# Context products of layer 2 in one unit of sixteen per half, nine probability buffers, and a new set of places

## The chip, the cores and the metric

The kernel runs on one core of one Trainium2 chip. The metric is the device time of one execution in microseconds (us); the number of a kernel is the median of its runs. The kernel before takes 3557.0 us (three runs, 3556.24 to 3559.87).

## The reference

There are 32 graphs of 512 nodes with 256 features in fp32, each with a symmetric adjacency matrix. Four graph layers follow one another, and each is wrapped as `x = layernorm(x + layer(x, adj))`. Layers 0, 1 and 3 are graph attention layers with additive logits. Layer 2 is a transformer block with masked attention over eight heads of 32, and it is the one that is changed:

```python
scores = einsum('bhqd,bhkd->bhqk', q * scale, k)
scores = where(allowed[:, None], scores, -inf)
attn = softmax(scores, axis=-1)
ctx = einsum('bhqk,bhkd->bhqd', attn, v)
x = layernorm(x + ctx @ Wo.T + bo)
x = layernorm(x + relu(x @ W1.T) @ W2.T)
```

## The kernel before

**Tiling.** A batch is one graph. Its 512 nodes are four row tiles of 128 (R = 4, index `j` or `r`), its 256 features two halves of 128 (K = 2, index `c`). Each half of layer 2 holds four heads. TensorE does the products and transposes, ScalarE (ACT) the exponentials and the copies out of PSUM, VectorE (DVE) masks, sums and statistics. Everything on the way from one layer to the next stays in SBUF, except the q and k of layer 2, which go over a DMA.

**Order.** A batch is a Python generator (`graph`), which yields a number, its place, before each unit of TensorE work. The place is `PERIOD * b + PLACES[stage][i]`, with the table in lines 28 to 48, and a merge by these numbers (`heapq.merge`) puts the units of several batches in one order. For TensorE this order is kept as it is (`manual_schedule`). The orders of ScalarE, VectorE and the DMA queue are set by the tile framework's scheduler. In the steady part, one period of 106.5 us holds the work of one batch, but of stages from different batches: layers 0 and 1 of a later batch run between the attention, feed forward and layer 3 of earlier ones.

**Names in the trace.** All products go through one helper, so they all carry line L104 and are told apart by their PSUM tiles: `h0p`, `h1p`, `h3p` are the features times weights of layers 0, 1, 3; `gp` spreads logits by transposes; `o` and `den` are the attention sums (`o<-pt,hv` and `den<-pt,hv` of layer 0 are column-tiled, 32 columns wide, four heads abreast; `o<-h,pt` are layers 1 and 3); `backp`, `xt1p`, `xt2p`, `xt3p`, `ytp` are transposes; `qkp` and `vp` make q, k and v; `s` are scores; `cp` are context products; `den<-pr,ones` are the sums of probabilities; `wop` is the projection; `f1p` and `f2p` are the feed forward.

**Attention of layer 2** (function `attention`). For each half `c`, and each row tile `j` and pair of heads `hp` in it, two products make scores `s` of 128x512; at `j = 3` a bf16 product adds the mask `shut` to them. ScalarE takes the exponential of each into a tile `pr` of 128x2x512 (L622). For `j < 3` VectorE multiplies that tile with the mask (L625). The context products read `pr` and `v` and accumulate in one PSUM bank `cp` per half, in four column tiles of 32, one per head. Before the change they are two units of eight per half, one after `j = 1` and one after `j = 3`, and the bank is taken at the half's start. After each unit VectorE adds the `pr` tiles of the two row tiles pairwise (`add_to`, L652). The halves of these sums are added later (`add_halves`), then `divide` multiplies with ones (`den`), takes the logarithm and exponential on ScalarE (L594 to L596), and scales the context `ct` on VectorE (L599). ScalarE's copy of `cp` to `ct` is L644.

**Buffers.** PSUM has one tag of eight banks (`bank`), which all products share in turn. `pr` has seven buffers. The `part` tag (128x512 scratch) has nine buffers in the first stage of a batch and six in the third.

**Other lines that the steps touch.** L280 normalises `y` on ScalarE with `rs` from L265, L266 (ScalarE) and L276 (VectorE), after the statistics `bn` (L273, L274). L421 is the exponential behind `h0p` that `gp` needs. L349 copies `gp` to `gb`, and L407 makes the layers' attention tiles `pt` from `gb` on VectorE. L695 is the activation `ft` between `f1p` and `f2p`. L709 to L711 add `f2p` to the second layernorm's `y`.

Of the kernel before, what the change touches and what calls it, by code (L numbers as in the profile page):

```python
# [9 lines left out]
F32 = mybir.dt.float32  # L10
# [15 lines left out]

PERIOD = 12054
PLACES = {
    "edges": [-3978, -1691, -957, 174],
    "x": [5375],  # L30
    "mask": [15529, 15550, 17375, 20858],
    "layer 0": [
        -32810, -32810, -32810, -32129, 5406, 5406, 5406, 5452, 8379, 10181, 10354, 11030,
        12979, 12979, 12979,
    ],
    "layer 1": [15397, 15397, 15551, 15551, 15637, 16368, 16395, 17082, 17350, 17359, 17359, 17361],
    "qkv": [17440, 17444, 22256, 22270, 23119, 23902, 25371, 25371, 25371, 25371, 25371],
    "attention": [
        -2905, -2905, -2905, -1865, 26410, 26425, 26425, 26425, 26478, 26596, 27423, 27447,
        27455, 27460, 28382, 28382, 28780, 28780, 29468, 30180, 32292, 32292, 33750, 33750,  # L40
    ],
    "projection": [34383, 34383, 34383, 34383, 35158],
    "feed forward": [
        35968, 36004, 36525, 37429, 38387, 38478, 38499, 38551, 38551, 38733, 38733, 39509,
        39509, 39647, 39706, 40498, 41141, 41450, 41519,
    ],
    "layer 3": [44306, 44306, 45121, 45121, 46359, 46359, 46477, 48020, 48020, 48023, 48398, 48528],
}
STAGES = {"edges": "a", "x": "a", "layer 0": "a", "layer 1": "a", "feed forward": "c", "layer 3": "c"}
ALL = mybir.DependencyInfo(mybir.DependencyClass.Sync, mybir.DependencyReason.DATA)  # L50
# [22 lines left out]
def fast_path(ctx: ExitStack, tc: tile.TileContext, a: dict, out: bass.AP, bad: bass.AP):  # L73
# [8 lines left out]
    nc = tc.nc  # L82
    B, N, D = a["x"].shape
    P = 128
    R = N // P
# [4 lines left out]
    DH = D // H2  # L90
# [12 lines left out]
    def product(what, *args, **kwargs):  # L103
        latest[0] = what(*args, **kwargs).ins.name  # L104
# [35 lines left out]
    v = const.tile([P, R, D], F32, name="v")  # L140
# [30 lines left out]
    def weights0():  # L171
        load_w(w0, "w0t")
        ab = part("a0")
        bcast(ab, "a0")
        bcast(bias0, "bias0")

        for s in range(2):
            prod = part("prod").rearrange("p (k d) -> p k d", k=K)
            nc.vector.tensor_mul(
                prod, w0[:, :, :D], ab[:, s * D : (s + 1) * D].unsqueeze(1).to_broadcast([P, K, D])  # L180
            )
            for k in range(K):
                nc.vector.tensor_reduce(
                    w0[:, k, D + s * H : D + (s + 1) * H],
                    prod[:, k, :].rearrange("p (h e) -> p h e", h=H),
                    axis=X,
                    op=ALU.add,
                )

    def weights13(w, name, vectors):  # L190
        load_w(w, name)
        ab = part(vectors)
        bcast(ab, vectors)
        for s in range(2):
            prod = part("prod").rearrange("p (k d) -> p k d", k=K)
            nc.vector.tensor_mul(
                prod, w[:, :, :D], ab[:, s * D : (s + 1) * D].unsqueeze(1).to_broadcast([P, K, D])
            )
            nc.vector.tensor_reduce(w[:, :, D + s], prod, axis=X, op=ALU.add)
# [45 lines left out]
    sb = ctx.enter_context(tc.tile_pool(name="sb", bufs=1))  # L245
    ps = ctx.enter_context(tc.tile_pool(name="ps", bufs=2, space=bass.MemoryType.PSUM))
    stage = ["a"]

    def buf(shape, tag, name, bufs, dtype=F32):

        return sb.tile(shape, dtype, tag=tag + stage[0], name=name, bufs=bufs)

    def bank(name, dtype=F32):
        shape = [P, 2048 // (2 if dtype == BF16 else 4)]
        return ps.tile(shape, dtype, tag="mm", name=name, bufs=8)

    def part(name):

        return buf([P, N], "part", name, {"a": 9, "c": 6}[stage[0]])

    def all_rows(v):
        return v.unsqueeze(1).to_broadcast([P, R, D])
# [312 lines left out]
    def attention(qk, a2, shut, spread):  # L575
        ct = buf([P, K, N], "ct", "ct", 1)
        pr = []

        def add_halves(pr):
            for hp in range(2):  # L580
                add_to(pr[0][hp], pr[2][hp])

        def divide(c, sums):
            den = bank("den")
            for hh in range(4):
                product(nc.tensor.matmul,
                    den[hh * DH : (hh + 1) * DH, :],
                    ones,
                    sums[hh // 2][:, hh % 2, :],
                    start=True,  # L590
                    stop=True,
                )
            t = buf([P, N], "dens", "dens", 2)
            nc.scalar.activation(t, den, AF.Copy, accum_out=spread[:, 2 * c : 2 * c + 1])  # L594
            nc.scalar.activation(t, t, AF.Ln)
            nc.scalar.activation(  # L596
                t, t, AF.Exp, scale=-1.0, accum_out=spread[:, 2 * c + 1 : 2 * c + 2]
            )
            nc.vector.tensor_mul(ct[:, c, :], ct[:, c, :], t)  # L599

        for c in range(K):
            cp = bank("cp")
            last, pr = pr, []
            for j in range(R):
                pr.append([])
                for hp in range(2):
                    yield
                    if last and (j, hp) == (1, 0):
                        add_halves(last)
                    t = sb.tile([P, 2, N], F32, tag="pr", name="pr", bufs=7)  # L610
                    for i in range(2):
                        s = bank("s")
                        product(nc.tensor.matmul,
                        s,
                            qk[2 * c + hp][:, 1, i, j * P : (j + 1) * P],
                            qk[2 * c + hp][:, 0, i, :],
                            start=True,
                            stop=j < R - 1,
                        )
                        if j == R - 1:  # L620
                            product(nc.tensor.matmul, s, identb, shut, start=False, stop=True)
                        nc.scalar.activation(t[:, i, :], s, AF.Exp, scale=QSCALE)  # L622
                    if j < R - 1:
                        edges = a2[:, j, :].unsqueeze(1).to_broadcast([P, 2, N])
                        nc.vector.tensor_mul(t, t, edges)  # L625
                    pr[j].append(t)
                if j % 2 == 0:
                    continue
                yield
                for jj in (j - 1, j):  # L630
                    for hh in range(4):
                        product(nc.tensor.matmul,
                        cp[hh * DH : (hh + 1) * DH, :],
                            v[:, jj, (4 * c + hh) * DH : (4 * c + hh + 1) * DH],
                            pr[jj][hh // 2][:, hh % 2, :],
                            start=jj == 0,
                            stop=jj == R - 1,
                        )
                for hp in range(2):
                    add_to(pr[j - 1][hp], pr[j][hp])  # L640
                if last and j == 1:
                    yield
                    divide(0, last[0])
            nc.scalar.copy(ct[:, c, :], cp)  # L644
        yield
        add_halves(pr)
        yield
        divide(1, pr[0])
        return ct

    def add_to(t, u):
        nc.vector.tensor_add(t, t, u)  # L652
# [830 lines left out]
```

## Time and profile before

| Quantity | Value |
|---|---|
| median of 3 runs | 3557.0 us (3556.24 to 3559.87) |
| profiled execution, its own time | 3556.76 us |
| its span | 3555.0 us |
| TensorE, products busy | 3422.4 us (96%) |
| TensorE, weight loads busy | 2385.6 us (67%) |
| VectorE busy | 2909.0 us (82%) |
| ScalarE busy | 2227.6 us (63%) |
| DMA queue q1, share of 16 engines | 33.6% |
| one period, from a context unit to the same one of the next batch (1498.79 to 1605.33 us) | 106.54 us |

The profile is of one execution. Busy times are sums over an engine's instructions. Products on TensorE overlap one another and their ends are modelled, so short pauses between them don't all show as idle time; they show in the starts. A line of the timeline is a run of equal instructions: its start, its length from the first start to the last end, engine, line, operation, output and inputs, shape, number, and in brackets an idle time ahead of it with what ended it. Each fp32 product shows as two records, a transpose as one.

### The profile page before, as it was taken

What the parts mean: (1) busy time and instruction counts of PE and PEld (TensorE: products, weight loads), DVE (VectorE), ACT (ScalarE), POOL (GpSimd) and SP (SyncE); (2) the same over time, 40 slices, a digit from 0 to 9 for tenths busy, and PEclk for the clock granted to TensorE, in tenths of its full rate; (3) what the DMA queues carried; (4) which work ended last, traced back from release to release, by engine and by line L of the source; (5) the groups of instructions that cost most, each with busy time, mean ns of one, the idle gap of its engine ahead of it and who ended that gap; (6) DMA issues with size and microseconds to landing.
All of it is one profiled execution on the core that took longest, in us unless ns stands there. A gap on an engine that the chain in (4) does not pass through costs nothing.

```text
span 3555.0 us, 51660 instructions
## 1 busy us (share of the span) xinstructions
PE 3422.4 (96%) x18278; PEld 2385.6 (67%) x18342; DVE 2909.0 (82%) x5178; ACT 2227.6 (63%) x5441; POOL 83.3 (2%) x171
## 2 busy tenths in 40 slices
PE   5899999999999999999999999999999999999986
PEld 3466666776666776666776666776666776676655
DVE  5788888888888888888888888888888888888763
ACT  3556666666666666666666666666666666666653
POOL 0000000000000000000000000000000000000000
PEclk8999999999999999999999999999999999999999
DMA  4334232334332234332334332334333234332120
GB/s 129 83 75 89 68 78 66 70 77 90 69 78 67 68 77 90 70 76 68 67 77 90 71 76 68 67 78 90 71 75 69 66 78 89 72 75 64 41 54 13
DMA packets 164040, 261.03 MB, mean 73 GB/s; under 512 B 20416, under 2 KB 56384, under 8 KB 163776
## 3 DMA queue, kind: packets, MB, share of 16 engines
q1 hardware_dynamic: 163776, 257.65, 33.6%
q8 instruction: 149, 2.44, 0.3%
q14 instruction: 115, 0.94, 0.1%
HBM read 106.57 MB, written 16.78 MB: 35 GB/s over the span
## 4 chain that ended last, share of the span: by engine, by line
PE 83%; DVE 10%; ACT 6%; DMA 1%; issue 1%; SPq 0%; ACTq 0%; DVEq 0%
PE o L104 14%; PE f2p L104 13%; PE f1p L104 12%; PE cp L104 7%; PE qkp L104 6%; PE s L104 6%; PE den L104 5%; PE h1p L104 3%; PE h3p L104 3%; PE wop L104 3%; PE vp L104 3%; DVE bn L273 3%; ACT y L280 2%; PE backp L104 1%; DVE relu L521 1%; DVE y L711 1%
## 5 line engine op out<-in xcount | busy, mean ns | idle before, releaser
L407 DVE SCALAR_TENSOR_TENSOR pt<-gb,ex,at 128x512 f32<-128x512 f32 x768 | 534.9, 740 | 51.3 <-ACT gb L349 48.8
L622 ACT ACTIVATE pr<-s 128x512 f32<-128x512 f32 x1024 | 537.4, 614 | 35.3 <-PE s L104 29.6
L652 DVE TENSOR_TENSOR pr<-pr 128x1024 f32<-128x1024 f32 x384 | 451.6, 1216 | 113.5 <-PE cp L104 113.1
L104 PE MATMUL f2p<-wf,ft 128*128 128x256 f32 x2048 | 491.3, 383 | 5.1 <-ACT ft L695 5.1
L625 DVE TENSOR_TENSOR pr<-pr,a 128x1024 f32<-128x1024 f32 x384 | 452.5, 1219 | 45.9 <-ACT pr L622 42.8
L104 PE MATMUL f1p<-yt,wf 128*128 128x256 f32 x2048 | 484.0, 379 | 2.4 <-ACT yt L320 0.2
L104 PE MATMUL o<-h,pt 128*128 128x257 f32 x2048 | 474.6, 381 | 5.4 <-DVE pt L407 3.8
L104 PEld LDWEIGHTS f2p<-wf,ft 128*128 128x128 f32 x2048 | 380.0, 189 | 110.8 <-issue 27.7
L104 PEld LDWEIGHTS o<-h,pt 128*128 128x128 f32 x2048 | 383.3, 190 | 75.8 <-issue 21.1
L695 ACT ACTIVATE ft<-f1p,cols 128x256 f32<-128x256 f32 x512 | 217.9, 471 | 342.6 <-PE f1p L104 339.0
L104 PEld LDWEIGHTS f1p<-yt,wf 128*128 128x128 f32 x2048 | 388.9, 190 | 54.5 <-ACT yt L320 0.7
L280 ACT ACTIVATE y<-y,rs 128x256 f32<-128x256 f32 x768 | 398.6, 593 | 11.2 <-DVE rs L276 11.1
L104 PE MATMUL s<-qk 128*128 128x512 f32 x1024 | 350.6, 458 | 4.4 <-DMA qk<-lo 2.1
L273 DVE BATCH_NORM_STATS2 bn<-y 128x6 f32<-128x256 f32 x768 | 298.3, 412 | 5.6
L104 PE MATMUL cp<-pr,v 128*32 128x512 f32 x2048 | 290.4, 609 | 2.6 <-ACT pr L622 1.1
L104 PE MATMUL o<-pt,hv 128*32 128x512 f32 x2048 | 279.9, 595 | 6.9 <-DVE pt L407 6.9
L104 PE MATMUL qkp<-xt,wqkv 128*128 128x512 f32 x512 | 233.6, 599 | 0.0
L104 PEld LDWEIGHTS s<-qk 128*128 128x128 f32 x1024 | 192.7, 191 | 36.5 <-issue 5.6
L548 DVE SCALAR_TENSOR_TENSOR lo<-qkp,cols,hi 128x512 fp32r<-128x512 f32 x128 | 95.6, 747 | 127.9 <-ACT hi L547 119.9
L349 ACT COPY gb<-gp 128x512 f32<-128x512 f32 x192 | 105.9, 586 | 125.5 <-PE gp L104 125.0
L104 PEld LDWEIGHTS qkp<-xt,wqkv 128*128 128x128 f32 x512 | 94.3, 189 | 121.3 <-issue 118.6
L104 PEld LDWEIGHTS o<-pt,hv 128*32 128x32 f32 x2048 | 87.1, 109 | 131.5 <-issue 77.4
(139 smaller groups left out, 4699.2 us busy)
## 6 DMA issues: line engine op xcount, KB each, us to landing
qk<-hi SPq DMA_DIRECT2D x512, 128.0 KB, 3.9
qk<-lo SPq DMA_DIRECT2D x512, 128.0 KB, 4.2
adjt<-in_adjt SPq DMA_DIRECT2D x64, 512.0 KB, 4.1
adj<-in_adj SPq DMA_DIRECT2D x64, 512.0 KB, 4.9
xt<-in_xt SPq DMA_DIRECT2D x32, 512.0 KB, 3.8
x<-in_x SPq DMA_DIRECT2D x32, 512.0 KB, 6.3
out<-y SPq DMA_DIRECT2D x32, 512.0 KB, 4.7
wf<-in_w1t SPq DMA_DIRECT2D x1, 1024.0 KB, 8.6
```

Of the source, the lines that this page charges most:

```text
L104: latest[0] = what(*args, **kwargs).ins.name
L273: nc.vector.bn_stats(st[:, r, :], y[:, r, :])
L280: nc.scalar.activation(y[:, r, :], y[:, r, :], AF.Identity, bias=rs[:, 1, r : r + 1], scale=rs[:, 0, r : r + 1],)
L349: nc.scalar.copy(g, p)
L407: nc.vector.scalar_tensor_tensor(t, g, f, edges, op0=ALU.max, op1=ALU.mult)
L521: nc.vector.scalar_tensor_tensor(y, m, 1.0, y, op0=ALU.min, op1=ALU.add)
L548: nc.vector.scalar_tensor_tensor(lo, p, bias, hi.bitcast(F32), op0=ALU.add, op1=ALU.subtract)
L622: nc.scalar.activation(t[:, i, :], s, AF.Exp, scale=QSCALE)
L625: nc.vector.tensor_mul(t, t, edges)
L652: nc.vector.tensor_add(t, t, u)
L695: nc.scalar.activation(ft[:, f, :], p[:, f, :], AF.Relu, bias=bf1[:, ff + f : ff + f + 1])
L711: nc.vector.tensor_mul(y, y, all_rows(ln2g))
```

## The change

- Per half, the context products become one unit of sixteen, after all four row tiles, and `cp` takes its bank only there. The four pairwise additions follow that unit. The place between `j = 1` and the division of the first half's context stays.
- `pr` gets nine buffers instead of seven.
- The third stage's `part` tag gets five buffers instead of six.
- `dynamic_dma_scratch_size` goes from 8192 to 512.
- `PLACES` has new numbers in all stages; `attention` has 22 instead of 24, one for each unit.
- From the attention function on, line numbers are smaller by one: L622, L625, L644, L652, L695 before are L621, L624, L643, L651, L694 after.

What this makes of TensorE's order in a steady period, from the order in which the changed program's instructions stand: the first half's sixteen come after its last scores and between feed-forward units, as the second of its two units did. The second half's sixteen come directly behind its last scores and ahead of `xt3p`; before, eight stood with `den<-pr,ones` in the stretch of the first half's division, and eight behind `xt3p` and ahead of layer 0's first `o`. Layer 0's `o` and `den` for `j = 1` come behind `den<-pr,ones`, and for `j = 0` behind `xt3p`, with six of the eight `h3p` and `xt2p` between.

```diff
 PLACES = {
-    "edges": [-3978, -1691, -957, 174],
+    "edges": [-6012, -1639, -513, 645],
...
     "attention": [
-        -2905, -2905, -2905, -1865, 26410, 26425, 26425, 26425, 26478, 26596, 27423, 27447,
-        27455, 27460, 28382, 28382, 28780, 28780, 29468, 30180, 32292, 32292, 33750, 33750,
+        -7028, -6668, -6668, -6033, 26498, 26498, 26498, 26605, 26607, 27394, 27394, 27474,
+        27474, 28393, 28791, 29214, 29504, 30179, 30179, 30179, 34315, 34319,
     ],
...
     def part(name):
 
-        return buf([P, N], "part", name, {"a": 9, "c": 6}[stage[0]])
+        return buf([P, N], "part", name, {"a": 9, "c": 5}[stage[0]])
...
         for c in range(K):
-            cp = bank("cp")
             last, pr = pr, []
...
-                    t = sb.tile([P, 2, N], F32, tag="pr", name="pr", bufs=7)
+                    t = sb.tile([P, 2, N], F32, tag="pr", name="pr", bufs=9)
...
                     pr[j].append(t)
-                if j % 2 == 0:
-                    continue
-                yield
-                for jj in (j - 1, j):
-                    for hh in range(4):
-                        product(nc.tensor.matmul,
-                        cp[hh * DH : (hh + 1) * DH, :],
-                            v[:, jj, (4 * c + hh) * DH : (4 * c + hh + 1) * DH],
-                            pr[jj][hh // 2][:, hh % 2, :],
-                            start=jj == 0,
-                            stop=jj == R - 1,
-                        )
-                for hp in range(2):
-                    add_to(pr[j - 1][hp], pr[j][hp])
                 if last and j == 1:
                     yield
                     divide(0, last[0])
+            yield
+            cp = bank("cp")
+            for jj in range(R):
+                for hh in range(4):
+                    product(nc.tensor.matmul,
+                        cp[hh * DH : (hh + 1) * DH, :],
+                        v[:, jj, (4 * c + hh) * DH : (4 * c + hh + 1) * DH],
+                        pr[jj][hh // 2][:, hh % 2, :],
+                        start=jj == 0,
+                        stop=jj == R - 1,
+                    )
+            for jj in (0, 2):
+                for hp in range(2):
+                    add_to(pr[jj][hp], pr[jj + 1][hp])
             nc.scalar.copy(ct[:, c, :], cp)
...
-    nc = bacc.Bacc("TRN2", target_bir_lowering=False, num_devices=1, dynamic_dma_scratch_size=8192)
+    nc = bacc.Bacc("TRN2", target_bir_lowering=False, num_devices=1, dynamic_dma_scratch_size=512)
```

## The prediction

> **What bounds the kernel now.** I read the first part of the page, then its slices and its chain, to see which engine sets the end.
>
> ```profile
> PE 3422.4 (96%) x18278; PEld 2385.6 (67%) x18342; DVE 2909.0 (82%) x5178; ACT 2227.6 (63%) x5441; POOL 83.3 (2%) x171
> PE   5899999999999999999999999999999999999986
> DVE  5788888888888888888888888888888888888763
> PE 83%; DVE 10%; ACT 6%; DMA 1%; issue 1%; SPq 0%; ACTq 0%; DVEq 0%
> ```
>
> TensorE is full in all but the first two and the last two slices, and the chain runs over it for 83%. So the time is TensorE's work plus its pauses. The changed program has the same number of matrix products, exponentials, multiplies and additions, so only pauses, mode changes and the two ends can change.
>
> The waits view tells little of the steady part, because pauses under the modelled ends of products do not show. I therefore read the timeline of TensorE in a middle stretch, by start times.
>
> ```profile
> 1498.79 2.42 PE L104 MATMUL cp<-pr,v 128*32 128x512 f32 x16
> 1501.13 1.99 PE L104 MATMUL f2p<-wf,ft 128*128 128x256 f32 x8
> ...
> 1511.00 1.92 PE L104 MATMUL cp<-pr,v 128*32 128x512 f32 x16
> 1512.85 1.99 PE L104 MATMUL f2p<-wf,ft 128*128 128x256 f32 x8
> ...
> 1551.31 1.96 PE L104 MATMUL gp<-ident,ex 128*128 128x128 f32 x16 [0.73 <-ACT ex L421]
> 1553.02 0.47 PE L104 MATMUL s<-qk 128*128 128x512 f32 x1
> ...
> 1554.02 0.41 PE L104 MATMUL xt3p<-ident,y 128*128 128x128 f32 x2
> 1554.59 0.33 PE L104 MATMUL xt3p<-ident,y 128*128 128x128 f32 x1 [0.16 <-ACT y L280]
> 1555.08 0.76 PE L104 MATMUL xt3p<-ident,y 128*128 128x128 f32 x5 [0.16 <-ACT y L280]
> 1555.78 2.15 PE L104 MATMUL cp<-pr,v 128*32 128x512 f32 x15
> ```
>
> The same context unit returns at 1605.33 and 1711.90 us, so a batch takes 106.54 us here. An fp32 product appears as two records. Undisturbed, one record of 128x256 follows the last after 0.216 us, one of 128x512 after 0.429, a transpose after 0.109, and four column-tiled records (32 wide, four heads abreast) after 0.427 together. What a block takes beyond this is a pause. The unit at 1511.00 takes 1.85 us to the next start, the one at 1498.79 takes 2.34. The transposes at 1554.02 take 1.76, where 8 x 0.109 plus a mode change of 0.1 would be 0.97. Read so, a period's pauses are:
> - 0.52 in the first context unit (last mask multiply L625),
> - 0.79 in xt3p (ScalarE's normalised y, L280),
> - 0.545 before xt2p (a PSUM bank that the copy L644 of cp frees),
> - 0.33 before h3p after the sums den(pr),
> - 0.89 before gp (ex L421).
>
> The sum is 3.07 us, which is near the 2.9% that a period's work leaves.
>
> **What the Trainium skill says.** "TensorEngine Tiling (Array Packing)", Tiling Modes, says that changing the tiling mode drains TensorE. The trace agrees: the last full product ahead of column tiles takes 0.309 instead of 0.216 us, the last group of tiles 0.522 instead of 0.409, and the next full block is late by about 0.105. That is 0.31 us for a stretch in and out. "Trainium Kernel Development and Optimization", Best Practices, says that consistent bubbles can mean that SBUF or PSUM ran out; the pause before xt2p, with a bank held by cp, is one. "VectorE: DVE Perf Modes", The DRAIN you can't avoid, says a next operation starts when the pipe has emptied. Here four additions of 128x1024 stand 4.62 us in the trace, 1.135 us from start to start, so a burst of them is not overlapped.
>
> **The change part by part.** Times are against the profiled run: 3556.76 us, span 3555.0, so 1.8 us lie around it; the median of the runs is 3557.0.
>
> *Half as many context units.* Per period four units of 8 products become two of 16. This looks like two fewer mode changes (0.62 us), but in the order before two of the four stood beside other column-tiled work (den(pr), o<-pt), and in the new order den and o stand split by xt2p, h3p and o3. Counted over the whole program, stretches of column mode go from 195 to 192. Three at 0.31 us: -1 us.
>
> *Pauses removed, per period.* The first unit no longer stands just behind its multiplies: -0.52. Context products now stand between the second half's scores and xt3p, where ScalarE's y (L280) was late: -0.79. cp's bank is taken only at the unit, and its copy comes before xt's two copies, with the o(j0) stretch and six h3p ahead of xt2p: -0.545. den(pr) is now followed by column-tiled o(j1), not h3p: -0.33. Sum -2.185. The pause before gp stays: h0p and L421 stand as they did.
>
> *Pauses added, per period.* Let g be the start of the layer-0 gp.
> 1. The second half's unit now comes directly behind its last scores. ScalarE's order (two gb, four y, two gb, rs, exponential, rs, exponential) is as before, where it ends at 1556.64 + 0.61, which is g + 5.94. TensorE wants it at g + 2.71 (start of xt3p before) + 0.1 + 6 x 0.427 = g + 5.37 for the last row tile's first group, or one group later if only the fourth head pair counts. Wait 0.63 with 0.06 of signal; at least 0.1. I take 0.63.
> 2. The four pair additions of the half, and two of the halves, are one burst of six on VectorE between the pt of j0 and of j1 (four stood there). VectorE is busy without a gap from 1543.8 to 1580. The burst starts as before at 1558.35, g + 7.04, and ends at g + 7.04 + 6 x 1.135 = 13.85; the four pt (L407) of j1 at 0.68 follow and the last is there at 16.5. TensorE comes to o(j1) at g + 15.25 (the new order's blocks summed, with 1) and wants the last pt 0.85 later: 0.52 with the signal. If TensorE is late there for any other cause, this goes to nothing.
> 3. f2p stands in one place behind f1p with only four transposes of backp between. Where they adjoin, at the end of the program, the trace has 0.727 us of wait for ft (L695, 0.471 us each); 4 x 0.109 covers part: 0.29.
> 4. The first half's context unit starts some 20 us after the last o<-h block; behind it f2p needs ft, which now stands behind rs L265 on ScalarE, and L265 waits for VectorE's statistics. These stand behind four of the half's additions, and those behind the context products. Nothing if the statistics are in time, up to about 1 us: 0.4.
> 5. o(j3) waits for pt that stand behind more additions: 0.1.
>
> Sum +1.94. Net -0.25 us a period. Steady periods run from about 270 to 3358 us, 29 of them: -7 us. Bounds: items 1, 2, 4 and 5 at nothing give -0.25 - 1.65 = -1.9 (rival A); 2, 4 and 5 at twice their size give +0.8, so +23 us.
>
> *Nine pr buffers, one part buffer fewer, a smaller DMA scratch.* A half now holds all eight tiles until its products are done, so nine are needed for the order at all; the ninth lets the next half's first tile begin. With eight live, the next half's first exponentials wait for a unit's additions; their items are in 2 and 5. The part tag of the second stage with five holds tiles of the feed forward and layer 3; the f1p items above include it. The DMAs all go by the hardware queue (q1, 33.6% of sixteen engines), whose share stays; scratch: 0.
>
> *Places, the head.* Until 211 us TensorE has about 81 us of pauses: xt1p waits 16.4 us for y, h0p 10.0 for w, o for pt. These belong to batch 0's chain of layers, which the edit does not shorten. Batch 0's context units waited some 17 us for scores and multiplies in all; grouping them saves a mode change and moves waits together: -2, from -6 to +4.
>
> *The tail.*
>
> ```profile
> 3455.04 2.80 PE L104 MATMUL xt3p<-ident,y 128*128 128x128 f32 x8 [9.04 <-ACT y L280]
> 3457.77 3.31 PE L104 MATMUL cp<-pr,v 128*32 128x512 f32 x16
> 3461.01 2.01 PE L104 MATMUL h3p<-w3g,xt 128*128 128x258 f32 x8
> ```
>
> In the last two batches xt3p waits 4.80 and 9.04 us for y, with context products behind it that had their inputs. All 16 now go ahead of it: 2 x 1.75 us fill the wait, so up to -3.5 each, -7. Against it, VectorE now adds inside the feed-forward's second layernorm (L711, bn): up to five additions of 1.135 us lie ahead of the statistics that y waits for, partly in VectorE's own idle time. I take +3. Tail -4, from -8 to +3.
>
> Sum: -1 - 7 - 2 - 4 = -14: 3543 us.
>
> **Rivals.**
>
> *A: the gaps close.* TensorE being late in one place covers the waits of another; only gp and item 3 are left. Then 29 x -1.9 = -55, ends and modes -7: 3495 us. For it: items 1, 2 and 5 are each under 0.7 us and lie behind one another, so a delay in 1 cancels 2. Against it: VectorE has no gap in this stretch, and the pauses of before summed to 3 us in a hand-set order too.
>
> *B: VectorE's first-half chain becomes the bound (slower).* Four additions and the four late multiplies (L625) surround backp's second y and layer 0's normalisation. If L265's statistics come over 1 us after ScalarE wants them, ft, y and the exponentials behind it are late in turn, and f2p, scores and xt1p each pause. Each us that the statistics are late costs TensorE a us per period. It decides from about 1.5 us late (0.25 + 0.4 + margin): at 2.5 us late, 2.1 more than item 4 holds, it is 29 x 1.85 - 7 = +47: 3604 us. For it: VectorE at 82%, and the additions waited for cp 113.1 us in all before, so a single unit makes them wait longer. Against: VectorE idles 15% of a period in its other part.
>
> *C: pauses only change place.* The net is within 0.25 us of nothing: 3550 to 3564, as 3557.
>
> **How the numbers follow.** Chances: the forecast (3515 to 3550) 0.42, A (under 3515) 0.17, C 0.18, B and other slower outcomes 0.23. Range: 3497 to 3590, leaving out about 0.1 on each side. Times under 3550 are faster by over 0.2% (7 us, about what measurement can tell here), those over 3564 slower: 0.59, 0.18, 0.23. The likeliest case's own range is 3515 to 3550.
>
> **What would show it.** TensorE's busy sum stays within 1%. The wait of xt3p for L280 falls to near nothing in a middle period, the first context unit has no pause, xt2p follows its block at once. A pause of 0.1 to 0.6 us stands at the last products of the second unit and at o(j1). The period is 106.3 us. In the tail, cp stands ahead of xt3p and its wait is shorter by about 3 us. Wrong would be: f2p, s or xt1p waiting on L695, L622 or L280 in each period (B), the head longer by over 10 us, or a period under 105.

## The result, and the profile after

The changed kernel takes 3535.2 us (four runs, 3533.34 to 3537.22), the one before 3556.7 us (four runs). The ratio is 0.9937, with a 95% interval of 0.9924 to 0.9949: 21.5 us faster, where 14 were forecast. The profiled execution took 3537.22 us with a span of 3535.4, so it is the longest of the four; that matters for the head, below.

The same parts of the page as before (busy time of each engine, slices, chain that ended last), of the changed kernel:

```profile
PE 3411.5 (96%) x18342; PEld 2358.3 (67%) x18342; DVE 2896.6 (82%) x5178; ACT 2219.6 (63%) x5441; POOL 82.6 (2%) x171
PE   6799999999999999999999999999999999999986
DVE  5678888888888888888888889888889888889763
PE 91%; DVE 3%; ACT 3%; issue 1%; DMA 1%; SPq 0%; POOL 0%; ACTq 0%; DVEq 0%; POOLq 0%
```

The numbers of instructions are the same (64 product records were missing before), and the shares hardly move. What tells something is the chain: TensorE carries 91% of it instead of 83%.

The timeline of TensorE in one middle period (start, length, operation), read by starts as before:

```profile
1505.84 3.64 PE L104 MATMUL cp<-pr,v 128*32 128x512 f32 x32
1509.41 1.99 PE L104 MATMUL f2p<-wf,ft 128*128 128x256 f32 x8
...
1546.16 1.96 PE L104 MATMUL gp<-ident,ex 128*128 128x128 f32 x16 [0.73 <-ACT ex L421]
...
1548.98 4.23 PE L104 MATMUL cp<-pr,v 128*32 128x512 f32 x32
1553.14 1.09 PE L104 MATMUL xt3p<-ident,y 128*128 128x128 f32 x8
1554.16 1.92 PE L104 MATMUL o<-pt,hv 128*32 128x512 f32 x16
...
1559.59 1.03 PE L104 MATMUL xt2p<-ident,y 128*128 128x128 f32 x8
1560.56 1.06 PE L104 MATMUL den<-pr,ones 128*32 128x512 f32 x8
1561.44 1.99 PE L104 MATMUL o<-pt,hv 128*32 128x512 f32 x14
...
1564.64 1.14 PE L104 MATMUL h3p<-w3g,xt 128*128 128x258 f32 x4
```

The first half's unit of 32 records takes 3.57 us to the next start: 32 x 0.1067 = 3.42 and a mode change, so no pause. The second half's takes 4.16, a pause of 0.59 for the last exponential: ScalarE ends it at 1552.11, and the records of the last head that need it follow at 1552.16. Then xt3p takes 1.02 us instead of 1.76. The `o` and `den` of row tile 1 together take 3.20 us; undisturbed they take 24 x 0.1067 = 2.56, and 0.12 to leave the column mode. So they pause 0.52 us.

The next first-half unit starts at 1611.65. A period is 105.81 us instead of 106.54.

From the starts of xt2p in the two traces, batch by batch, the 19.6 us between the spans divide so: the head puts the changed kernel 6.4 us behind, the 27 periods from batch 3 to batch 30 bring 19.0, and the tail 7.0.

### The profile page after: what moved, and what is told of

The parts are those of the page before. It is cut to its first block, busy times and chain, and to the rows that moved or that the text cites. A ratio compares the mean times of both kernels' runs of the same rounds, so it can differ in the third digit from the quotient of the medians.

```text
span 3535.4 us, 51325 instructions
## 1 busy us (share of the span) xinstructions
PE 3411.5 (96%) x18342; PEld 2358.3 (67%) x18342; DVE 2896.6 (82%) x5178; ACT 2219.6 (63%) x5441; POOL 82.6 (2%) x171
## 4 chain that ended last, share of the span: by engine, by line
PE 91%; DVE 3%; ACT 3%; issue 1%; DMA 1%; SPq 0%; POOL 0%; ACTq 0%; DVEq 0%; POOLq 0%
PE o L104 18%; PE f2p L104 13%; PE f1p L104 12%; PE s L104 8%; PE cp L104 6%; PE qkp L104 6%; PE den L104 5%; PE h3p L104 4%; PE h1p L104 3%; PE vp L104 3%; PE wop L104 3%; PE h0p L104 3%; PE gp L104 2%; PE xt3p L104 1%; PE xt1p L104 1%
## 5 line engine op out<-in xcount | busy, mean ns | idle before, releaser
L624 DVE TENSOR_TENSOR pr<-pr,a 128x1024 f32<-128x1024 f32 x384 | 455.1, 1219 | 123.8 <-ACT pr L621 123.4
L621 ACT ACTIVATE pr<-s 128x512 f32<-128x512 f32 x1024 | 541.1, 614 | 5.7 <-PE s L104 2.2
L651 DVE TENSOR_TENSOR pr<-pr 128x1024 f32<-128x1024 f32 x384 | 450.1, 1210 | 1.9 <-PE cp L104 1.9
L694 ACT ACTIVATE ft<-f1p,cols 128x256 f32<-128x256 f32 x512 | 217.8, 472 | 309.2 <-PE f1p L104 307.5
L104 PE MATMUL s<-qk 128*128 128x512 f32 x1024 | 361.9, 464 | 6.0 <-DMA qk<-lo 6.0
L104 PE MATMUL o<-pt,hv 128*32 128x512 f32 x2048 | 270.7, 601 | 4.2 <-DVE pt L407 4.2
L104 PE MATMUL cp<-pr,v 128*32 128x512 f32 x2048 | 251.7, 596 | 1.4 <-DVE pr L624 1.4
L104 PE MATMUL qkp<-xt,wqkv 128*128 128x512 f32 x512 | 242.4, 597 | 0.0
L265 ACT ACTIVATE rs<-mvs,eps1e-05_70 128x4 f32<-128x4 f32 x192 | 57.5, 300 | 257.0 <-DVE mvs L274 251.1
L740 DVE RECIPROCAL rd<-o 128x1 f32<-128x1 f32 x128 | 21.5, 168 | 208.4 <-PE o L104 206.8
L104 PEld LDWEIGHTS o<-pt,hv 128*32 128x32 f32 x2048 | 65.6, 109 | 168.4 <-issue 102.1
L104 PEld LDWEIGHTS cp<-pr,v 128*32 128x32 f32 x2048 | 63.9, 109 | 145.6 <-issue 123.8
```

The costliest lines, as they stand in the source:

```text
L265: nc.scalar.activation(out, variance, AF.Ln, bias=eps[e])
L694: nc.scalar.activation(ft[:, f, :], p[:, f, :], AF.Relu, bias=bf1[:, ff + f : ff + f + 1])
L740: nc.vector.reciprocal(rd[:, r : r + 1], p[:, D : D + 1])
```

## The experiments

All kernels but e10 keep every operation. Periods are the distance of the same block in successive batches. Each ratio is to runs of the kernel before that were taken with that experiment; their medians lie between 3557.0 and 3558.2 us.

**Which part of the change makes it faster.** First the buffers alone: the kernel before with nine `pr` buffers, five `part` buffers in the third stage and a scratch of 512. The first of these edits:

```diff
-                    t = sb.tile([P, 2, N], F32, tag="pr", name="pr", bufs=7)
+                    t = sb.tile([P, 2, N], F32, tag="pr", name="pr", bufs=9)
...
```

> The kernel before with the three buffer edits alone (pr nine, third-stage part five, small DMA scratch); TensorE's order is as before. Theory 1: no pause of before is one for a pr tile, so 3554 to 3560. Rival (more probability buffers let scores run ahead and shorten pauses by themselves): under 3550.

3557.7 us, ratio 1.0001 (0.9992 to 1.0010). The buffers alone do nothing that these runs show.

Then the changed code with the places of before, without the entries of the two units that fell away:

```diff
-        -2905, -2905, -2905, -1865, 26410, 26425, 26425, 26425, 26478, 26596, 27423, 27447,
-        27455, 27460, 28382, 28382, 28780, 28780, 29468, 30180, 32292, 32292, 33750, 33750,
+        -2905, -2905, -2905, -1865, 26425, 26425, 26425, 26478, 26596, 27423, 27447,
+        27455, 27460, 28382, 28780, 28780, 29468, 30180, 32292, 32292, 33750, 33750,
...
```

> The one unit of sixteen per half and the buffers of the change, with the places of before (the two entries of the dropped units taken out). In this order the second half's sixteen products stand behind xt3p, not ahead of it. Theory 1 (the gain is a sum of pauses, and the pause of xt3p goes only because products stand ahead of it): the pause of the first context unit goes (-0.52 us a period) and one mode change with it (-0.31), xt3p keeps its 0.8 us, o(j1) may gain 0.2 to 0.5; 3535 to 3548 us, and xt3p's idle time for L280 stays over 30 us in all. Rival (the new places alone do it, the merging is nothing): 3553 to 3560.

3597.7 us, ratio 1.0111 (1.0094 to 1.0128). Both were wrong: it is 40 us slower, and the period is 107.96. The timeline of TensorE shows where (here the helper is line 103):

```profile
1513.60 1.89 PE L103 MATMUL f1p<-yt,wf 128*128 128x256 f32 x8
1516.05 1.99 PE L103 MATMUL f2p<-wf,ft 128*128 128x256 f32 x8 [0.56 <-ACT ft L693]
...
1523.12 1.99 PE L103 MATMUL f2p<-wf,ft 128*128 128x256 f32 x8 [0.57 <-ACT ft L693]
...
1581.73 2.61 PE L103 MATMUL o<-pt,hv 128*32 128x512 f32 x14
...
1585.56 2.01 PE L103 MATMUL h3p<-w3g,xt 128*128 128x258 f32 x8
```

The unit that was taken out had stood between an f1p and its f2p, and had covered ScalarE's `ft`. Now that f1p takes 2.45 us to the next start instead of 1.73. From this `ft` to the next one (1516.26 to 1523.4) ScalarE works without a gap, where it had 0.55 us to spare before, so the following f2p is 0.73 us late too: 1.46 us a period. xt3p kept its wait, as expected (35.1 us in all). With the products behind xt3p the additions come late, and `o` and `den` of row tile 1 take 3.83 us, a pause of 1.15 instead of 0.33; the sums of probabilities, den(pr), pause 0.3. Less the two pauses that went (0.52, 0.55), that is +1.5 us a period against +1.4 measured. I had counted only what left, not what the removed unit had been covering.

The reverse: the new places and buffers with two units of eight, the first of each half at its old relative place.

```diff
-            yield
-            cp = bank("cp")
-            for jj in range(R):
+                if j % 2 == 0:
+                    continue
+                yield
+                for jj in (j - 1, j):
...
```

> The new places and buffers with two units of eight per half as before (the first unit of each half back at its old relative place, the bank taken at the half's start). Theory 1: only eight products now cover the wait of xt3p, and their last row tile is wanted about 0.85 us after the unit's start, while the last exponential ends as late as ever: the pause in that unit grows from 0.6 to about 2.3 us, and the first half's extra unit pays a mode change of 0.31; 3535 + 29 x 2.0 = about 3593, range 3570 to 3600. Rival (new places alone): 3532 to 3540.

3592.4 us, ratio 1.0098 (1.0081 to 1.0115), and the period is 107.8, 2.0 over that of the changed kernel.

```profile
1570.33 1.91 PE L103 MATMUL cp<-pr,v 128*32 128x512 f32 x12
1572.94 1.63 PE L103 MATMUL cp<-pr,v 128*32 128x512 f32 x4 [0.70 <-ACT pr L621]
1574.49 1.09 PE L103 MATMUL xt3p<-ident,y 128*128 128x128 f32 x8
```

The short unit takes 4.16 us where 1.71 and a mode change are its work: 2.30 us of pause for the last exponential, as expected from ScalarE's order. So neither half of the change is of use alone (+40, +35 us): at the new place eight products are done too soon to hide the last exponential, and sixteen leave a pause of only 0.59.

**Was it the bank?** The changed kernel with `cp` taken at the half's start again:

```diff
         for c in range(K):
+            cp = bank("cp")
             last, pr = pr, []
...
-            cp = bank("cp")
             for jj in range(R):
```

> The changed kernel with the bank cp taken at each half's start again, as before; TensorE's order stays. My prediction put the pause before xt2p (0.545 us a period before) down to the bank that cp holds. Theory 1 as amended (it went because 16 more blocks stand between, that is by the order, and seven banks are enough elsewhere): 3533 to 3538, no pause before xt2p. Rival (holding the bank for a half costs by itself): 3543 to 3551, with pauses at blocks that wait for a bank.

3535.8 us (3532.99 to 3538.48) against 3535.2, and xt2p follows its block as in the changed kernel. Holding the bank early costs nothing that these runs show.

The bank had not made the pause of before either. TensorE's timeline of before, behind the line at 1555.78 of the prediction, and ScalarE's:

```profile
1557.52 0.68 PE L104 MATMUL o<-pt,hv 128*32 128x512 f32 x3
1557.76 0.59 PE L104 MATMUL cp<-pr,v 128*32 128x512 f32 x1
1557.95 1.69 PE L104 MATMUL o<-pt,hv 128*32 128x512 f32 x12
...
1560.86 1.09 PE L104 MATMUL xt2p<-ident,y 128*128 128x128 f32 x8
```

```profile
1556.64 0.61 ACT L622 ACTIVATE pr<-s 128x512 f32<-128x512 f32 x1
...
1560.07 0.58 ACT L644 COPY ct<-cp 128x512 f32<-128x512 f32 x1
```

The last exponential ends at 1557.25, and only then, at 1557.31 and 1557.76, do the fourth head's last two records of `cp` start; the first head's last stands at 1557.09. The fourth head's six records of `o` and `den` follow 0.43 us apart, the last at 1560.33, and xt2p comes 0.52 later, the ordinary time of a last group of column tiles. So nothing waits directly before xt2p: what was read as a pause there is the wait of the fourth head for the last exponential, carried along its column. The last record stands 0.52 us before xt2p in every batch from 1 to 30. In batch 1, where the exponentials are early, it is 4.43 us from the start of the unit to xt2p; in the steady periods it is 5.08. The copy L644 ends 0.2 us ahead of xt2p, and so the views of the profile name it.

**What holds the period at 105.8 us.** The changed kernel still pauses at gp (0.89) and in the second unit (0.59). Moving the half's last scores ahead of gp fills the first and brings the exponentials sooner for the second.

```diff
-        27474, 28393, 28791, 29214, 29504, 30179, 30179, 30179, 34315, 34319,
+        27474, 28393, 28791, 29214, 29504, 29507, 30179, 30179, 34315, 34319,
...
-        -36706, -36616, -36616, -36025, 1272, 1272, 1272, 1272, 8879, 10211, 11116, 11129,
+        -36706, -36616, -36616, -36025, 5400, 5400, 5400, 5400, 8879, 10211, 11116, 11129,
```

> The changed kernel with the last scores of the second half moved ahead of layer 0's gp transposes, which wait about 0.8 us for the exponential L421. Theory 1 (that wait is latency of one chain and can be filled; and the exponentials that the sixteen products wait 0.6 us for come earlier): gp's pause falls to under 0.2 us and the pause in the unit to under 0.2, -1.2 us a period, 3535 - 35 = about 3500, range 3490 to 3515. Rival (ScalarE then does two exponentials before the copies gb, so pt and o come late and the pause comes back there): 3530 to 3550, with o<-pt waiting for L407 in each period.

3534.2 us (3531.47 to 3534.34): the median lies within the changed kernel's own runs. The rival was right. The timeline of TensorE:

```profile
1545.13 1.94 PE L104 MATMUL gp<-ident,ex 128*128 128x128 f32 x16
1547.00 3.64 PE L104 MATMUL cp<-pr,v 128*32 128x512 f32 x32
1550.57 1.09 PE L104 MATMUL xt3p<-ident,y 128*128 128x128 f32 x8
1551.59 2.45 PE L104 MATMUL o<-pt,hv 128*32 128x512 f32 x14
...
1555.26 2.88 PE L104 MATMUL h3p<-w3g,xt 128*128 128x258 f32 x12
```

The pauses at gp and in the unit are gone, but row tile 0's `o` and `den` take 3.67 us (pause 0.99), and row tile 1's 3.76 (pause 1.08). In all 2.07 us; in the changed kernel 0.89 + 0.59 + 0.52 = 2.00, and the period is 105.8 in both. The timeline of VectorE in this kernel shows what they wait for:

```profile
1549.46 1.19 DVE L651 TENSOR_TENSOR pr<-pr 128x1024 f32<-128x1024 f32 x1
...
1550.64 2.73 DVE L407 SCALAR_TENSOR_TENSOR pt<-gb,ex,at 128x512 f32<-128x512 f32 x4
1553.29 5.75 DVE L651 TENSOR_TENSOR pr<-pr 128x1024 f32<-128x1024 f32 x5
1558.97 2.72 DVE L407 SCALAR_TENSOR_TENSOR pt<-gb,ex,at 128x512 f32<-128x512 f32 x4
```

From layer 1's relu (L521, at 1537.62) to 1563.5 VectorE has no gap. Its list there ends with row tile 1's `pt`, and TensorE can't pass `o` of row tile 1 before it. A pause of TensorE anywhere ahead of that is slack.

If that is so, taking additions out of the list must pay. In the next two kernels the second half's six additions are issued after the `pt` of row tile 1, and its den(pr) comes after `o` of row tile 1.

```diff
-            for jj in (0, 2):
-                for hp in range(2):
-                    add_to(pr[jj][hp], pr[jj + 1][hp])
+            if c == 0:
+                add_pairs(pr)
             nc.scalar.copy(ct[:, c, :], cp)
         yield
+        add_pairs(pr)
         add_halves(pr)
...
-        27474, 28393, 28791, 29214, 29504, 30179, 30179, 30179, 34315, 34319,
+        27474, 28393, 28791, 29214, 29504, 30179, 30179, 33000, 34320, 34320,
```

`add_pairs` is the loop that was taken out. First on the changed kernel:

> The changed kernel with the second half's six additions issued after layer 0's pt of row tile 1 and its den(pr) after o(j1), to take them out of the way of the pt on VectorE. Theory 2, formed from the look at e5 (from layer 1's end to o(j1), VectorE has no gap, so TensorE can't pass o(j1) sooner than VectorE's queue lets it; pauses ahead of it are only its slack): o(j1) no longer waits (0.52 us a period), the pauses at gp and in the second unit stay; 3535 - 29 x 0.5 = 3520, range 3515 to 3526. Rival (the wait then stands at den(pr) or wop, which need the additions): 3530 to 3540.

3516.5 us, ratio to before 0.9884 (0.9867 to 0.9900). The period is 105.3, and row tile 1 no longer waits:

```profile
1550.78 1.93 PE L104 MATMUL o<-pt,hv 128*32 128x512 f32 x16
1552.52 1.04 PE L104 MATMUL den<-pt,hv 128*32 128x512 f32 x8
1553.38 1.04 PE L104 MATMUL den<-pr,ones 128*32 128x512 f32 x8
```

That is 2.60 us, and the pauses at gp and in the unit stand as they were. VectorE's timeline shows that only three of the six additions moved; the scheduler leaves the other three ahead of the last `pt` of row tile 1:

```profile
1544.10 3.48 DVE L656 TENSOR_TENSOR pr<-pr 128x1024 f32<-128x1024 f32 x3
1547.51 2.07 DVE L407 SCALAR_TENSOR_TENSOR pt<-gb,ex,at 128x512 f32<-128x512 f32 x3
1549.49 3.49 DVE L656 TENSOR_TENSOR pr<-pr 128x1024 f32<-128x1024 f32 x3
```

Then together with the early scores:

> Both e5's early scores and e6's late additions. e5 alone gave 3534: the 1.5 us that it took from gp and the unit came back as 1.0 at o(j0) and 1.1 at o(j1). Theory 2: with the additions out of the way only the wait at o(j0) is left of these, so 3534 - 29 x 1.05 = 3504, range 3495 to 3512, and more than the two edits' gains alone (1 + 15). Rival (no shared bound; the edits add up): 3519 or later.

3512.6 us (3511.29 to 3517.76), ratio 0.9876 (0.9859 to 0.9892), period 105.1. The early scores take 0.02 us off the period alone (the median from batch 3 to 30 goes from 105.82 to 105.80) and 0.20 with the additions late (105.31 to 105.10), so the edits do share a bound. In time that is 1 and 4 us, with runs that overlap. The gain is 8 us short of what I gave. The pause at row tile 0 stays (1541.17 to 1544.85, 3.68 us), because the scheduler still puts one addition ahead of row tile 0's `pt`, and den(pr) now waits 0.2 us for the last addition.

```profile
1539.03 1.19 DVE L656 TENSOR_TENSOR pr<-pr 128x1024 f32<-128x1024 f32 x1
...
1540.21 3.40 DVE L407 SCALAR_TENSOR_TENSOR pt<-gb,ex,at 128x512 f32<-128x512 f32 x5
```

To see how far VectorE's list is the cause, the additions of the second half were left out of that kernel, so that its sums of probabilities are those of a constant:

```diff
         yield
-        add_pairs(pr)
-        add_halves(pr)
         yield
-        divide(1, pr[0])
+        plain = ones[:, :1].unsqueeze(1).to_broadcast([P, 2, N])
+        divide(1, [plain, plain])
```

> e7 without the six additions of the second half (left out; its sums of probabilities are then those of a constant, so this part of the result is not computed). e7 stayed 8 us behind what I gave for it: one addition still stands ahead of row tile 0's pt on VectorE and o(j0) waits 1.0 us, and den(pr) waits 0.33 for the last. Theory 2 (VectorE's queue up to those pt is the bound): the rest of both goes, 3512.6 - 29 x (1.0 + 0.3) = 3475, range 3470 to 3490, and o(j0)'s stretch takes 2.7 us as in the changed kernel. Rival (o(j0) waits for ScalarE's copies gb, which come behind two exponentials): o(j0) still waits 0.8 us or more and the time stays over 3498.

3492.1 us (3487.48 to 3492.99), period 104.6. Row tile 0 and the sums after row tile 1:

```profile
1533.48 2.14 PE L104 MATMUL o<-pt,hv 128*32 128x512 f32 x16
1535.23 1.26 PE L104 MATMUL den<-pt,hv 128*32 128x512 f32 x8
1536.41 2.88 PE L104 MATMUL h3p<-w3g,xt 128*128 128x258 f32 x12
...
1542.70 1.04 PE L104 MATMUL den<-ones 128*32 128x512 f32 x8
1543.67 1.14 PE L104 MATMUL h3p<-w3g,xt 128*128 128x258 f32 x4
```

The pause at row tile 0 falls from 1.00 to 0.25 us and that at den goes, so the additions on VectorE were most of it. The time lies between the two theories' ranges, 2 us above that of VectorE: of the 1.0 us gained there, 0.5 comes back as a pause between wop and qkp, where the trace names VectorE's L548, and 0.1 behind it. This kernel takes the work away and not only its place, and what L548 waits for was not tried.

**The head.** For batch 1 alone, the last layer-0 transposes backp go back to the place of the other eight.

```diff
-            yield PERIOD * b + PLACES[name][min(i, len(PLACES[name]) - 1)]
+            place = PLACES[name][min(i, len(PLACES[name]) - 1)]
+            if b == 1 and place == 13658:
+                place = 13325
+            yield PERIOD * b + place
```

> The changed kernel with one place changed for batch 1 only: its last layer-0 transposes backp stand with the other eight, ahead of vp, as they did before, not behind the first scores of batch 0. The head was 6 us longer after the change, where I had 2 us less. Theory 1: those transposes came some 8 us later, so layer 0's normalisation, which xt1p waits for with nothing else to do, began later on VectorE; 3531 to 3533 (2 to 4 us less), the steady part unchanged. Rival (six additions instead of four among that chain on VectorE): 3534.5 to 3536.

3532.6 us (3530.22 to 3534.21), 2.6 less, with runs that overlap those of the changed kernel, and the period is unchanged. xt1p of batch 1 starts at 136.60 us instead of 138.06. In this trace xt2p of batch 3 stands 0.1 us ahead of before, and in e9's, with the same place, 0.2 behind. Where the place is that of the changed kernel and no operation is missing, it stands behind by 2.6 to 2.7 us (e4, e6, e7), 5.3 (e5) and 6.4 (the changed kernel, e2). So the transposes' place makes the head longer by about 2.5 us or more, and moving it back takes this away. What makes 2.6 into 6.4 stays open. Nor is it the only thing that counts: e10 keeps the place, has xt1p of batch 1 at 138.00, and still stands 0.8 ahead of before at batch 3.

**A faster version.** e7 with that one place:

> The best of the versions so far: e7 (early scores, late additions, 3512.6) with the head's one place of e8 (2.6 us less). They touch different stretches, so they should add: 3510, range 3508 to 3512. If the head's gain was only slack of what follows: 3512.6.

3507.9 us (3506.96 to 3508.76), ratio to before 0.9861 (0.9845 to 0.9878). It is 4.7 us under e7 where 2.6 were expected; with runs of e7 between 3511.3 and 3517.8 the two edits add, or a little more.

## Why the prediction was right, and where it was off

The direction held, and so did the frame: the time is a sum of TensorE's pauses, their balance is negative, and the two large terms, the first unit and xt3p, are as forecast. The size was 21.5 us against 14, and the total hides larger differences: the steady part brought 19.0 us over 27 periods, where 29 were to bring 7, the head lost time where it was to gain 2, and the tail brought 7 instead of 4. By the steps, a period:

| Step | Predicted, us | Measured, us |
|---|---|---|
| first unit behind its multiplies | -0.52 | -0.52 |
| xt3p | -0.79 | -0.74 |
| xt2p | -0.545 | -0.55 (not a wait of xt2p) |
| h3p | -0.33 | not removed |
| item 1, second unit | +0.63 | +0.59 |
| item 2, o(j1) | +0.52 | +0.19 (0.33 to 0.52) |
| item 3, f2p behind backp | +0.29 | +0.29 |
| item 4, first-half chain | +0.40 | 0 |
| item 5, o(j3) | +0.10 | 0 |
| net | -0.25 | -0.74 by steps, -0.73 by the two periods above, -0.70 in the mean from batch 3 to 30 |

**Items 4 and 5 failed.** They were guesses without a wait of before to lean on, and put 0.5 us x 29 = 14 us on the wrong side. f2p starts 3.57 us after the first unit's start, with no pause. Rival B was this item grown large. On ScalarE L265 does wait longer for VectorE's statistics (251.1 us in all, before 86.8), but between f1p and f2p it cost TensorE nothing. No run here made that queue late enough to try B.

**Two pauses were named wrongly, and both cancelled.** I put 0.33 us down to h3p behind den(pr). In the trace of before, row tile 1's `o` and `den` start at 1564.51 and h3p at 1567.52: 3.01 us for 2.68 of work. So it was o(j1) waiting for its last `pt`, the same wait as item 2, which grew to 0.52. I had taken 0.33 off and put 0.52 on; the balance, +0.19, was right by accident. The reading matters all the same: a pause that had been VectorE's all along was the first sign of the bound that e5 to e10 show, and my sum treated it as two unrelated things.

The other is xt2p and item 1. Both are the wait of the context products for the second half's last exponential (see e4): 0.55 us before, or 0.65 by the fourth head's own records, and 0.59 after. I had taken 0.545 off for a bank and put 0.63 on for the exponential; the balance, +0.09 against +0.04, was right by accident too. So of the four pauses that were to go, two went, and the other two stayed with the blocks that they belong to.

**The bank.** The Trainium skill says in "Trainium Kernel Development and Optimization", Best Practices, that consistent bubbles can mean that PSUM ran out. I took the pause before xt2p for one of these. The trace does not agree: xt2p follows the last record ahead of it after the ordinary 0.52 us, and holding the bank longer leaves the time where it was (e4).

**Item 3** holds to 0.01 us: backp's four records take 0.73 us to the next start (1601.05 to 1601.78) for 0.44 of work.

**Mode changes.** The 1 us for three of them stays an estimate; no run isolates it. The steps above account for the steady part to about 0.1 us a period without it.

**Head and tail.** Head: predicted -2; measured +6.4 in the profiled execution and +2.6 to +6.4 in the other traces of that place. The step that failed is that the waits up to 211 us were all put down to batch 0's chain, which the edit does not change. The xt1p that starts at 136.32 us, after 4.83 us of idle time, is batch 1's; in the changed kernel it starts at 138.06 after 8.30. The place of batch 1's backp delays the normalisation that it waits for (e8). Tail: predicted -4, measured -7.0. The xt3p that waited 4.80 us comes 5.7 us earlier against before than the one ahead of it, more than the 3.5 given; cp's pause of 1.9 us behind it goes too. The one that waited 9.04 gains 0.1 only: here the additions on VectorE cost all of the 3.5, where I had taken 3. From there to the end another 3.1 is gained and 1.6 lost, which I had not foreseen and did not follow. TensorE's and VectorE's timelines around the second of these, in the changed kernel,

```profile
3423.59 3.64 PE L104 MATMUL cp<-pr,v 128*32 128x512 f32 x32
3436.97 2.80 PE L104 MATMUL xt3p<-ident,y 128*128 128x128 f32 x8 [9.75 <-ACT y L280]
```

```profile
3428.17 1.22 DVE L710 TENSOR_TENSOR y<-y,ln2g_b 128x1024 f32<-128x1024 f32 x1
3429.31 1.21 DVE L651 TENSOR_TENSOR pr<-pr 128x1024 f32<-128x1024 f32 x1
3430.44 1.22 DVE L711 TENSOR_TENSOR y<-y,y 128x1024 f32<-128x1024 f32 x1
3431.58 1.22 DVE L651 TENSOR_TENSOR pr<-pr 128x1024 f32<-128x1024 f32 x1
```

show the additions (L651) between the steps of the chain that y waits for (here L710 scales y, and L711 adds x to it), so the wait is 9.75 us though sixteen products stand ahead of it.

**Rival A** (late in one place covers another, and the sum shrinks) saw that the pauses trade with one another. But they trade because VectorE's list is fixed, so covering one moves it, and the sum stays (e5).

## What to carry to other kernels

A removed unit is two things: its own cost, and the cover that it gave to the wait behind it. Before moving one, name what stood behind it (e1: 1.46 us a period at two places).

Pauses of the bounding engine may be the slack of another engine's list. Sum the pauses between two points that the other engine fixes; if an edit keeps that sum (2.00 and 2.07 us here), it has moved them, and what pays is to shorten what the other engine has to do ahead of the second point (e6: 19 us from moving three additions a period behind that point, on an engine that is 82% busy over the whole span).

A pause that is seen where a block starts may have begun earlier. Where several heads run abreast, follow the records of one of them: here a wait of one head travelled 3 us along its column and looked like a wait of the next block.

## What was not expected of the hardware

Nothing in an operation's time: 1.135 us from one addition of 128x1024 to the next (each lasts 1.21, so they overlap by 0.08), 0.1067 us for a column-tiled record and 0.109 for a transpose served for every trace read here. The head is what differs between traces of the same order, by about 4 us (the place of batch 3's xt2p against before: +6.4 in the changed kernel's trace, +2.6 in e4's). So a gain in the head of less than that is read from the timed runs and not from one trace.
